# Giving every engine a written order of work in a fused graph-attention layer

## The chip, the cores and the metric

The kernel runs on one core of a Trainium2 chip. The metric is the device time of one execution in microseconds (us). The engines are TensorE (PE, with its weight loads PEld), VectorE (DVE), ScalarE (ACT), GpSimd (POOL) and SyncE (SP), which here only issues DMA transfers.

## The reference

The input x is 128 x 128 x 768, 128 graphs of 128 nodes, in float32; adj is 128 x 128 x 128. Cut to what matters:

```
h = relu(layernorm(x))                         # over the last axis, eps 1e-5
q, k, v = h @ Wq + bq, h @ Wk + bk, h @ Wv + bv  # 12 heads of 64
scores = q @ k^T / 8 + beta * adj
scores = where(adj > 0, scores, -9e15)
out = x + softmax(scores) @ v                  # heads put side by side again
```

## The kernel before

The work is cut into 32 groups of four graphs. For each group the three projections are done in three **slices**: `qk0` (q and k of the first six heads), `v`, and `qk1` (q and k of the other six). A slice is a product of 2 x 3 blocks of activations with 3 x 3 blocks of weights, each block 256 wide, and it is done with 15 block products (`PRODUCTS`) in place of 18. The inputs of these products are sums of blocks: `sum_acts` (DVE) makes the sums of activations, named S, and the sums of weights, named T, are made once.

In the qk0 and v slices each block product is itself done with 7 instead of 8 products of half blocks (`product_z`, 28 matmuls at L494). Its weights are seven 128 x 128 parts that are prepared once in group 0 (`prepare`), stored to DRAM (`kept`, L259 and L285) and loaded again for every product (`load_T`, L305), 448 KB each. A ring of five buffers (`RING`) holds them; the load for the product five places on is issued when a product has freed its buffer. The activations' inner sums, named SP, are made by POOL (`inner`, L426 to L429), four operations for each product. The results of a slice are kept in encoded form and decoded by POOL (`decode`, L537 to L540 for q and k, L548 to L553 for v) before they are used. A product's result is taken out of its PSUM bank by ACT where it is the first for an output block, and added by DVE otherwise (L519, L520); the next product of the same chain (there are four chains, each with its own banks) needs that bank free.

The qk1 slice uses plain block products (`product`, L568) with weights that stay in SBUF. Group 0 runs qk0 and v with plain weights (`plain_slice`, L768), while the weights are prepared.

Beside the slices, written into a dictionary `todo` from the number of a block product to functions, go:

- the attention of the group: `scores` (L604, L608, L611) and `attend` (L641), whose steps are put between matmuls; its end scales the result (L625), adds x on POOL (L650) and stores it (L651). The x for that is loaded by `load_xo` (L592)
- the layer norm of the next group: x is loaded in transposed blocks (`load_x`, L169), normalized by ACT (`norm`, L408) and transposed by DVE (`to_hT`, L414). From the third group on, the statistics come from x by rows (`load_halves`, `row_stats` at L383, `row_moments` at L394 and L395) and are turned to the blocks' order by 16 small transfers (`block<-row`, L399)
- the bias from adj (`load_adj` L436, `bias_1`, `bias_2`, L441 to L458).

Apart from the startup all transfers are issued by SP, in the order in which they stand in its program. The order in which the engines get these instructions is set by the framework's scheduler, by priority and its own estimate of times; `tc.issue_after` puts single instructions behind others. So products of the qk1 slice are found inside the v slice of the profile.

Of the kernel before, what the change touches and what calls it, by code (L numbers as in the profile page):

```python
# [31 lines left out]
def kernel(  # L32
# [25 lines left out]
    with tc.If(again > 0):  # L58
# [56 lines left out]
HT_AT = {"A01": 0, "A00": 1, "A11": 2, "A02": 3, "A10": 4, "A12": 9}  # L115
SUMS_AT = (5, 9, 6, 6, 7, 8, 9, 10, 11, 13, 14)
INNER_AT = ((5, (1, 11, 12)), (6, (0,)), (7, (4, 2)), (8, (5,)), (9, (6,)), (10, (8, 3, 9)), (11, (7,)), (12, (10,)),
            (14, (13, 14)))


@with_exitstack
def direct(ctx, tc, x, adj, wq, bq, wk, bk, wv, bv, beta, out, bad):
# [42 lines left out]
    def load_x(G, g, engines):  # L165
        t = home_x(G, g)
        src = x[G * GRP + g].rearrange("(b i) (a f) -> a i b f", i=SQ, a=NB)
        for a in range(NB):
            engines[a % len(engines)].dma_start(t[a * SQ:(a + 1) * SQ], src[a])  # L169
# [26 lines left out]
    def load_part(w, k, at, n, t):  # L196
        src = w.rearrange("(a c j) n -> a j c n", a=NB, j=SQ)
        for a in range(NB):
            nc.sync.dma_start(t[a * SQ:(a + 1) * SQ], src[a][:, 2 * k:2 * k + 2, at:at + n])

    def load_block(sl, k, j, t):
        if sl == "v":
            load_part(wv, k, j * 2 * P, 2 * P, t)
        else:
            for i, w in enumerate((wq, wk)):
                load_part(w, k, (j + 3 * int(sl[2])) * P, P, t[:, :, i * P:(i + 1) * P])
# [3 lines left out]
    def load_weights(sl, blocks=[f"B{k}{j}" for j in range(3) for k in range(3)]):  # L210
        for b in blocks:
            if sl == "qk1":
                t = const.tile([P, 2, H2], F32, name=f"{sl}_{HOME.get(b, b)}")
            else:
                n = nraw[0]
                nraw[0] += 1
                if n < len(PRODUCTS):
                    t = work.tile([P, GRP, P], F32, tag=f"SP{n}", name=f"{sl}_{b}", bufs=1)
                else:
                    t = work.tile([P, GRP, P], F32, tag="xo", name=f"{sl}_{b}", bufs=3)  # L220
                t = t.rearrange("p (c i) n -> p c (i n)", c=2)
            load_block(sl, int(b[1]), int(b[2]), t)
            wt[sl, b] = t
# [83 lines left out]
    load_weights("qk0", ["B00", "B10", "B20"])  # L307
    for g in range(2, GRP):
        load_x(0, g, (nc.sync,))
# [76 lines left out]
    def row_moments(G):  # L386
# [10 lines left out]
        for b in range(NB):  # L397
            for a in range(NB):
                nc.sync.dma_start(to[a * SQ:(a + 1) * SQ, b], t[b * SQ:(b + 1) * SQ])  # L399
# [39 lines left out]
    def bias_1(G, raw):  # L439
        a = work.tile([P, GRP, N], F32, tag="adjT", name=f"adjT_{G}", bufs=1)  # L440
        nc.vector.transpose(a, raw.rearrange("p g b j -> p g (b j)"))  # L441
# [3 lines left out]
        t = biasT[G] = work.tile([P, GRP, N], F32, tag="biasT", name=f"biasT_{G}", bufs=2)  # L445
        nc.gpsimd.memset(t, MASKED)
        nc.vector.copy_predicated(t, kp, a)
        if G:
            square(a)
        return a  # L450

    def square(a):
        nc.scalar.activation(a, a, AF.Square, scale=1.0005 * math.sqrt(SUM_CAP) / (BIAS_CAP * ISCALE))

    def bias_2(G, a):
# [6 lines left out]
    between = deque()  # L462
# [18 lines left out]
    def product_z(G, sl, n):  # L481
# [15 lines left out]
        load_T()  # L497
        for (r, j), sign in uses:
# [23 lines left out]
            if not left[key]:  # L522
                decode(G, sl, r, j)
        if n == mine[-1]:
            for b in banks.pop(chain):
                give(b)

# [27 lines left out]
    def product(G, sl, n, order):  # L555
# [8 lines left out]
        for i in range(2):  # L564
            for c in range(2):
# [4 lines left out]
                turn()  # L570
        for (r, j), sign in uses:
# [13 lines left out]
        if n == mine[-1]:  # L585
            give(banks.pop(chain))

# [44 lines left out]
    def attend_steps(G, oc):  # L632
# [17 lines left out]
        nc.gpsimd.tensor_add(t, t, o.rearrange("p a (b j) d -> p (a b) (j d)", j=2))  # L650
        nc.sync.dma_start(out[G * GRP:(G + 1) * GRP, :, oc * P:(oc + 1) * P].rearrange("g n d -> n g d"), t)  # L651
# [80 lines left out]
    def attention(G, u, at=AV_AT):  # L732

        todo = {}
        for i, oc in enumerate((3 * u + 2, 3 * u, 3 * u + 1)):
            todo.setdefault(at[i] - 3, []).append(lambda oc=oc: load_xo(G, oc))
            todo.setdefault(at[i], []).append(lambda oc=oc: attend(G, oc))
        return todo

    def slice_z(G, sl, todo):  # L740
        for at, n in enumerate(ZORDER):
            product_z(G, sl, n)
            for f in todo.get(at, ()):
                f()

    def slice_of(G, sl, todo, order=range(len(PRODUCTS))):
        for at, n in enumerate(order):
            product(G, sl, n, order)
            for f in todo.get(at, ()):
                f()  # L750

    def plain_slice(G, sl, todo):

        n = 0
        for r in range(2):
            for j in range(3):
# [4 lines left out]
                for at, k in [(at, k) for at in parts for k in range(3)]:  # L761
# [28 lines left out]
                    for f in todo.get(n, ()):  # L790
                        f()
                    n += 1


    adj_0 = load_adj(0)
# [96 lines left out]
    def behind_adds(f, *args):  # L892

        with tc.issue_after(added[0].ins):
            return f(*args)

    def behind_scores(f, *args):

        with tc.issue_after(taken[0].ins):
            return f(*args)  # L900

# [5 lines left out]
    early, raw = [], []  # L907
    for G in range(NG):
        todo = attention(G - 1, 1, AV_Z) if G else {}

        def then(n, f):
            todo.setdefault(n, []).append(f)

        def behind(f, *args):

            with tc.issue_after(added[G].ins):
                return f(*args)

        if G:
            for n, order in ((1, (2, 0)), (2, (1,))):  # L920
                todo.setdefault(n, []).insert(0, lambda order=order: scores(G - 1, 1, order))

        if G + 1 < NG:
            for g in range(GRP):
                then(6, lambda g=g: load_x(G + 1, g, (nc.sync,)))
                if G == 1:
                    then(11 + g, lambda g=g: behind_scores(stats, G + 1, g))
                elif G:
                    then((0, 5, 8, 11)[g], lambda g=g: load_halves(G + 1, g))
                    then((4, 7, 10, 13)[g], lambda g=g: behind(row_stats, G + 1, g))  # L930
            if G > 1:
                raw = []
                then(14, lambda: raw.append(load_adj(G + 1)))
                then(14, lambda: row_moments(G + 1))
        if not G:
            load_weights("qk1", AS_SUMMED)
            then(0, lambda: behind_rows(half, 0))
            then(3, lambda: half(1))
            then(4, lambda: half(2))
            prep = deque(prepare("qk0") + prepare("v"))  # L940

            def step(behind, count):
                for _ in range(count):
                    if prep:
                        behind(prep.popleft())

            for n in range(5, 18):
                then(n, lambda n=n: step(after, 1 + n % 2))
            plain_slice(0, "qk0", todo)
        else:  # L950
            if G == 1:
                then(4, lambda: behind_scores(bias_2, 1, early[1]))
            slice_z(G, "qk0", todo)
        todo = {1: [lambda: scores(G, 0, (2, 0))], 2: [lambda: scores(G, 0, (1,))]} if G else {}
        if G + 1 < NG:
            got = []
            at = 3 if G else 5
            for g in range(GRP):
                if not G:
                    then(g, lambda g=g: stats(G + 1, g))  # L960
                if G or g < 2:
                    then(at + 5 + g, lambda g=g: behind(norm, G + 1, g) if G > 1 else norm(G + 1, g))
            if G < 2:
                then(at, lambda: got.extend(moments_1(G + 1, 0, GRP * NB)))
                then(at + (3 if G else 2), lambda: moments_2(G + 1, 0, GRP * NB, *got[:2]))
            if G:
                then(8, lambda: got.append(behind(bias_1, G + 1, raw.pop()) if raw else bias_1(G + 1, load_adj(G + 1))))
                then(12, lambda: bias_2(G + 1, got[-1]))
            else:
                for n in range(len(SUMS_B)):  # L970
                    then(n + 3, lambda n=n: behind_adds(sum_weights, "qk1", n))
                for n in range(len(SUMS_A)):
                    then(n + 4, lambda n=n: sum_acts(0, n))
                for n in range(18):
                    then(n, lambda: step(lambda f: f(), 2))
                then(10, lambda: early.append(behind_adds(bias_1, 0, adj_0)))
        if G:
            slice_z(G, "v", todo)
        else:
            plain_slice(0, "v", todo)  # L980
        todo = attention(G, 0)
        if not G:
            todo.setdefault(SC_AT, []).insert(0, lambda: scores(0, 0))

        def transposes(n):
            with tc.issue_after(added[G].ins if G else taken[0].ins):
                to_hT(G + 1, int(n[1]), int(n[2]))

        def behind_opened(f, *args):

            with tc.issue_after(opened[0].ins):
# [175 lines left out]
```

## Time and profile before

| | |
|---|---|
| median of 2 runs (lowest, highest) | 3589.33 us (3587.52, 3591.14) |
| the profiled execution | 3600.97 us |
| its span, first to last instruction | 3599.0 us |
| granted TensorE clock, mean | 0.912 |
| PE busy | 2921.5 us, 81% |
| POOL busy | 2334.8 us, 65% |
| DVE busy | 2114.0 us, 59% |
| ACT busy | 1361.9 us, 38% |
| DMA | 660.86 MB, mean 184 GB/s, 57.6% of 16 engines |
| first matmul with prepared weights (group 1) | 206.2 us |
| first qk0 matmul of group 2 and of group 31 | 299.1 us and 3485.1 us |

Times inside the profile are microseconds from the first instruction of that execution. A line of a group reads: line of the code, engine, operation, what it writes and reads, number | busy time, mean ns of one | idle time of the engine before them and what ended it. A line of waits reads: who waits, for whom: total us, times, longest. A timeline line reads: start, duration, engine and line, what; SPq is the issue of a transfer.

### The profile page before, as it was taken

To read this page: it belongs to the slowest core of one execution; us is meant where nothing else is said; L and a number is where in the kernel's file an instruction comes from. 1 tells how busy PE (TensorE), PEld (TensorE's weight loads), DVE (VectorE), ACT (ScalarE), POOL (GpSimd) and SP (SyncE) were. 2 spreads that over 40 slices of the span, in tenths; PEclk is the share of its full clock that TensorE was granted. 3 is DMA by queue.
4 is the path that set the end of the run, shared out by engine and by line. 5 is a ranking of instruction groups with operands and counts; after the bars stand their busy time and mean duration, and the time that the engine had idled before them with its cause. 6 is when DMAs were issued, how large, how long until landed. Compare 5 with 4: busy or idle time off the path is not lost.

```text
span 3599.0 us, 114220 instructions
## 1 busy us (share of the span) xinstructions
PE 2921.5 (81%) x46385; PEld 2519.5 (70%) x46385; DVE 2114.0 (59%) x4755; ACT 1361.9 (38%) x3999; POOL 2334.8 (65%) x4146
## 2 busy tenths in 40 slices
PE   8478878778888788787787887787877878878878
PEld 7377767667677767676676777676776767776767
DVE  3556656556565566565565655565655756556655
ACT  1234343343343443334433433433344334344333
POOL 1757766568676677665686766676656867567764
PEclk9779999899999999999999999998988999999999
DMA  3485655756556656557565566565575655665644
GB/s 96 155 250 168 204 168 184 223 166 195 170 168 218 192 168 207 158 189 222 170 197 177 164 213 204 164 209 159 180 223 165 198 173 164 217 191 170 207 142 154
DMA packets 552487, 660.86 MB, mean 184 GB/s; under 512 B 126348, under 2 KB 428696, under 8 KB 551960
## 3 DMA queue, kind: packets, MB, share of 16 engines
q1 hardware_dynamic: 551632, 653.13, 57.6%
q8 instruction: 367, 6.01, 0.7%
q14 instruction: 160, 1.31, 0.1%
q10 hardware_dynamic: 328, 0.40, 0.1%
HBM read 588.78 MB, written 64.09 MB: 181 GB/s over the span
## 4 chain that ended last, share of the span: by engine, by line


## 5 line engine op out<-in xcount | busy, mean ns | idle before, releaser
L494 PE MATMUL bank<-SP,T_qk 128*64 128x128 f32 x7440 | 709.5, 288 | 46.9 <-POOL SP L428 46.9
L494 PE MATMUL bank<-T_v,SP 128*64 128x128 f32 x7440 | 679.3, 285 | 0.0
L625 ACT ACTIVATE o<-bank,sm 128x64 f32<-128x64 f32 x1524 | 348.4, 318 | 849.2 <-DVE sm L619 448.9
L494 PE MATMUL bank<-S,T_qk 128*64 128x128 f32 x4092 | 445.4, 295 | 244.3 <-DMA T_qk<-kept_qk 243.5
L494 PE MATMUL bank<-T_v,S 128*64 128x128 f32 x4092 | 432.8, 293 | 221.0 <-DMA T_v<-kept_v 219.4
L519 DVE TENSOR_TENSOR qk<-qk,bank 128x512 f32<-128x512 f32 x310 | 208.5, 672 | 559.0 <-PE bank L494 391.0
L548 POOL TENSOR_TENSOR v<-v 128x128 f32<-128x128 f32 x186 | 85.3, 459 | 681.3 <-DVE v L519 681.3
L494 PEld LDWEIGHTS bank<-SP,T_qk 128*64 128x64 f32 x7440 | 482.9, 147 | 53.0 <-POOL SP L428 53.0
L641 PEld LDWEIGHTS bank<-v,e 128*64 128x64 f32 x6048 | 407.2, 138 | 128.0 <-ACT o L625 11.6
L494 PEld LDWEIGHTS bank<-T_v,SP 128*64 128x64 f32 x7440 | 486.4, 145 | 0.0
L494 PEld LDWEIGHTS bank<-S,T_qk 128*64 128x64 f32 x4092 | 281.4, 150 | 261.5 <-issue 254.5
L494 PEld LDWEIGHTS bank<-T_v,S 128*64 128x64 f32 x4092 | 275.1, 148 | 247.0 <-DMA T_v<-kept_v 228.0
L568 PE MATMUL bank<-S,qk_T 128*64 128x256 f32 x3584 | 442.2, 380 | 2.6 <-DVE qk L583 1.7
L641 PE MATMUL bank<-v,e 128*64 128x65 f32 x6048 | 432.3, 222 | 13.2 <-ACT o L625 7.0
L537 POOL TENSOR_TENSOR qk<-qk 128x256 f32<-128x256 f32 x186 | 135.8, 730 | 325.4 <-DVE qk L519 325.2
L577 ACT ACTIVATE qk<-bank,bqk 128x256 f32<-128x256 f32 x384 | 164.2, 473 | 362.5 <-POOL v L553 158.9
L583 DVE TENSOR_TENSOR qk<-qk,bank 128x512 f32<-128x512 f32 x321 | 219.1, 683 | 137.6 <-PE bank L568 116.5
L568 PE MATMUL bank<-A,qk_T 128*64 128x256 f32 x2048 | 253.4, 384 | 48.3 <-ACT v L509 41.2
L608 DVE SCALAR_TENSOR_TENSOR e<-bank,biasT 128x512 f32<-128x512 f32 x378 | 237.9, 684 | 89.6 <-PE bank L604 88.7
L568 PE MATMUL bank<-S,qk_B 128*64 128x256 f32 x2048 | 278.8, 384 | 13.5 <-DVE qk L583 12.7
L568 PEld LDWEIGHTS bank<-S,qk_T 128*64 128x64 f32 x3584 | 231.1, 137 | 82.5 <-DVE qk L583 1.8
L408 ACT ACTIVATE x<-x,block 128x192 f32<-128x192 f32 x464 | 217.9, 536 | 138.3 <-DMA block<-row 133.2
(157 smaller groups left out, 5934.1 us busy)
## 6 DMA issues: line engine op xcount, KB each, us to landing
T_qk<-kept_qk SPq DMA_DIRECT2D x465, 448.0 KB, 5.0
T_v<-kept_v SPq DMA_DIRECT2D x465, 448.0 KB, 4.7
x<-in_x_dram SPq DMA_DIRECT2D x504, 96.0 KB, 2.8
xo<-in_x_dram SPq DMA_DIRECT2D x189, 256.0 KB, 5.3
out_dram<-xo SPq DMA_DIRECT2D x189, 256.0 KB, 2.6
half<-in_x_dram SPq DMA_DIRECT2D x232, 192.0 KB, 4.7
adj<-in_adj_dram SPq DMA_DIRECT2D x128, 64.0 KB, 3.1
block<-row SPq DMA_DIRECT2D x464, 1.0 KB, 1.7
```

Source lines behind the costliest of these rows:

```text
L408: nc.scalar.activation(t, t, AF.Relu, bias=shift[G, n], scale=rstd[G, n])
L494: nc.tensor.matmul(p[z // 4][q:q + HD, z % 4, :], lhs[:, q:q + HD], rhs, start=(first and z % 4 == 0), stop=True, skip_group_check=True)
L519: nc.vector.tensor_tensor(t[:, 0:4], t[:, 0:4], p[0], op)
L537: e.tensor_tensor(t[:, 1:4:2], t[:, 1:4:2], twice(0), ALU.add)
L548: e.tensor_tensor(v[:, 0:2, 0:HD], heads(0), heads(3), ALU.add)
L568: nc.tensor.matmul(p[q:q + HD, i, :], lhs[:, q:q + HD], rhs, start=(first and i == 0 and c == 0), stop=(c == 1), skip_group_check=True)
L577: opened[0] = nc.scalar.activation(t[:, i, :], p[:, i, :], AF.Identity, bias=bqk[:, i, oc:oc + 1], scale=float(sign))
L583: added[G] = nc.vector.tensor_tensor(t[:, :, cols], t[:, :, cols], p[:, :, cols], ALU.add if sign > 0 else ALU.subtract)
L608: taken[0] = nc.vector.scalar_tensor_tensor(e, ps[oc, i].rearrange("p (g n) -> p g n", g=GRP), SCORE_CAP * ISCALE, biasT[G], op0=ALU.min, ...
L625: nc.scalar.activation(o[:, b], pa[:, b, 0:HD], AF.Copy, scale=t[:, 1, b:b + 1])
L641: nc.tensor.matmul(pa[q:q + HD, 2 * g + i, :], es[G, oc, i][:, 2 * r + g, q:q + HD], vt[G, "v", r, h // 4][:, 4 * g + h % 4, :], start=Tru ...
```

## The change

The framework's scheduler keeps only the first slice of group 0 and the last slice of the last group. Between them, under `tc.manual_schedule()`, every engine runs its instructions in the order in which the program states them. A slice is run by slots, one for each block product: first the product's matmuls and (in qk0 and v) the issue of the next T load, then the slot's `todo`, then what earlier slots put off, then the taking out of the product's result, then what is marked "post":

```
+    def later(f, slots=1):
+        while len(deferred) < slots:
+            deferred.append([])
+        deferred[slots - 1].append(f)
+
+    def overdue():
+        if deferred:
+            for f in deferred.popleft():
+                f()
...
+    def run(products, todo):
+        for at, steps in enumerate(products):
+            next(steps)
             for f in todo.get(at, ()):
                 f()
+            overdue()
+            next(steps)
+            for f in todo.get((at, "post"), ()):
+                f()
```

The decoding of an output block, the addition of x and the store are put off by one, one and two slots:

```
             if not left[key]:
-                decode(G, sl, r, j)
+                later(lambda r=r, j=j: decode(G, sl, r, j))
...
-        nc.gpsimd.tensor_add(t, t, o.rearrange("p a (b j) d -> p (a b) (j d)", j=2))
-        nc.sync.dma_start(out[G * GRP:(G + 1) * GRP, :, oc * P:(oc + 1) * P].rearrange("g n d -> n g d"), t)
+
+        def add():
+            nc.gpsimd.tensor_add(t, t, o.rearrange("p a (b j) d -> p (a b) (j d)", j=2))
+
+        def send():
+            nc.sync.dma_start(out[G * GRP:(G + 1) * GRP, :, oc * P:(oc + 1) * P].rearrange("g n d -> n g d"), t)
+
+        later(add)
+        later(send, 2)
```

x is loaded for two graphs by one set of four transfers, a weight block by two transfers of 128 partitions instead of four of 32 (the first three blocks on the queues of SP and ACT), and the row statistics are turned by way of DRAM:

```
-    def load_x(G, g, engines):
-        t = home_x(G, g)
-        src = x[G * GRP + g].rearrange("(b i) (a f) -> a i b f", i=SQ, a=NB)
+    def load_x(G, r):
+        for g in range(2):
+            home_x(G, 2 * r + g)
+        src = x[G * GRP + 2 * r:G * GRP + 2 * r + 2].rearrange("g (b i) (a f) -> a i (g b) f", i=SQ, a=NB)
         for a in range(NB):
-            engines[a % len(engines)].dma_start(t[a * SQ:(a + 1) * SQ], src[a])
+            nc.sync.dma_start(xp[G, r][a * SQ:(a + 1) * SQ], src[a])
...
-        src = w.rearrange("(a c j) n -> a j c n", a=NB, j=SQ)
-        for a in range(NB):
-            nc.sync.dma_start(t[a * SQ:(a + 1) * SQ], src[a][:, 2 * k:2 * k + 2, at:at + n])
+        src = w.rearrange("(a c j) n -> c a j n", a=NB, j=SQ)
+        for c in range(2):
+            engine.dma_start(t[:, c], src[2 * k + c][:, :, at:at + n])
...
-        for b in range(NB):
-            for a in range(NB):
-                nc.sync.dma_start(to[a * SQ:(a + 1) * SQ, b], t[b * SQ:(b + 1) * SQ])
+        turned = dram.tile([SQ, NB, 2 * GRP], F32, name=f"turned_{G}")
+        nc.sync.dma_start(turned.rearrange("i b s -> b i s"), t.rearrange("p s g -> p (s g)"))
+        nc.sync.dma_start(to.rearrange("p b s g -> p (b s g)"),
+                          turned.rearrange("i b s -> i (b s)")[None].to_broadcast([NB, SQ, NB * 2 * GRP]))
```

The bias is cut into four steps (`bias_steps`). The slots of the regular groups, from the third on (`then(slot, function, ...)`, `activations` and `attention` fill the same dictionary):

```
+    def activations(G, first):
+        for name, at in (("A01", 3), ("A00", 5), ("A02", 6), ("A11", 9), ("A10", 17), ("A12", 24)):
+            if at >= 15:
+                then(at - 15, to_hT, G, int(name[1]), int(name[2]))
...
+        for n, at in enumerate((2, 10, 3, 5, 6, 7, 11, 12, 13, 14)):
+            then(at, sum_acts, G, n)
+        for n, at in ((0, 3), (1, 3), (2, 4), (11, 4), (12, 5), (4, 6), (5, 7), (6, 8), (8, 10), (3, 11), (7, 12), (9, 13),
+                      (10, 14), (13, 14)):
+            then(at, inner, G, n)
...
# qk0 of group G (more: a further group follows)
+        then(0, sum_acts, G, 10)
+        then(1, inner, G, 14)
+        for n, order in ((1, (2, 0)), (2, (1,))):
+            then((n, "post"), scores, G - 1, 1, order)
+        attention(G - 1, 1, AV_Z)
...
+        elif more:
+            then(0, row_moments, G + 1)
+            then(0, add_raw, G + 1)
+            bias(G + 1, 3, 5, 6, 12)
# v of group G
+        for n, order in ((1, (2, 0)), (2, (1,))):
+            then((n, "post"), scores, G, 0, order)
+        if more:
+            for g in range(GRP):
+                then((0, 2, 4, 6)[g], norm, G + 1, g)
+            for name, at in (("A01", 4), ("A00", 5), ("A02", 6), ("A11", 9)):
+                then(at, to_hT, G + 1, int(name[1]), int(name[2]))
...
+                then(13, load_halves, G + 2, 0)
# qk1 of group G
+        attention(G, 0, AV_AT)
+        activations(G + 1, False)
+        if G + 2 < NG:
+            for g, at in enumerate((1, 4, 8, 12)):
+                then(at, row_stats, G + 2, g)
+                if g < 3:
+                    then(at, load_halves, G + 2, g + 1)
+            for r, at in enumerate((6, 11)):
+                then(at, load_x, G + 2, r)
```

`add_raw` issues the four loads of adj; `attention(G, u, at)` puts the load of x for the sum three slots ahead of each of its three `attend`, at slots 7, 9, 12 (`AV_Z`) and 5, 8, 11 (`AV_AT`). Before, x of the next group was loaded at slot 6 of qk0, the row halves at slots 0, 5, 8 and 11 and `row_moments` and the adjacency at slot 14 of qk0, the normalizations stood at slots 8 to 11 and the bias at 8 and 12 of v.

## The prediction

> **What bounds the kernel now.** I read the page's table of engines first. TensorE (PE) is busy 81% of the span, so some 680 us of idle time are to be found. The page's list of groups says what ends them: the first matmuls of a block product wait for the load of a prepared weight T, 244 us in the qk0 slices and 219 us in the v slices.
>
> ```profile
> PE 2921.5 (81%) x46385; PEld 2519.5 (70%) x46385; DVE 2114.0 (59%) x4755; ACT 1361.9 (38%) x3999; POOL 2334.8 (65%) x4146
> ...
> L494 PE MATMUL bank<-S,T_qk 128*64 128x128 f32 x4092 | 445.4, 295 | 244.3 <-DMA T_qk<-kept_qk 243.5
> L494 PE MATMUL bank<-T_v,S 128*64 128x128 f32 x4092 | 432.8, 293 | 221.0 <-DMA T_v<-kept_v 219.4
> ```
>
> Then the busy times by stretch for one middle group, from its first qk0 matmul to the next group's, cut where PE stops and starts (columns: stretch, length, busy us of PE, PEld, DVE, ACT, POOL, granted clock, DMA share, GB/s):
>
> ```profile
> 1835.90:1848.90 13.00, 11.35 (x240) 10.14 (x235) 6.75 (x13) 9.49 (x30) 12.61 (x26) 1.00 0.34 95
> 1848.90:1856.60 7.70, 0.03 (x2) 0.06 (x2) 2.00 (x5) 0.20 (x1) 5.28 (x11) 0.68 0.76 223
> 1856.60:1877.40 20.80, 20.80 (x376) 20.63 (x378) 13.35 (x37) 7.39 (x28) 11.79 (x16) 0.87 0.94 314
> 1877.40:1889.90 12.50, 11.21 (x242) 10.28 (x240) 9.04 (x27) 7.17 (x17) 8.68 (x13) 1.00 0.67 191
> 1889.90:1903.40 13.50, 3.80 (x36) 2.02 (x31) 0.83 (x2) 7.71 (x17) 0.00 (x0) 0.85 0.25 68
> 1903.40:1920.50 17.10, 16.97 (x278) 16.58 (x280) 12.26 (x24) 3.62 (x9) 10.12 (x21) 0.92 0.89 301
> 1920.50:1945.90 25.40, 25.40 (x312) 17.88 (x310) 21.21 (x46) 7.07 (x24) 24.46 (x45) 1.00 0.34 104
> 1835.90:1945.90 110.00, 89.55 (x1470) 77.59 (x1467) 65.43 (x149) 42.65 (x125) 72.94 (x130) 0.92 0.60 187
> 243.50:270.40 26.90, 26.63 (x514) 25.66 (x511) 20.67 (x48) 16.10 (x35) 17.69 (x28) 1.00 0.90 283
> 270.40:299.10 28.70, 28.70 (x342) 20.02 (x339) 22.21 (x48) 8.74 (x28) 27.60 (x54) 1.00 0.35 106
> ```
>
> A group takes 110 us and has two holes of 7.7 us, in the second and fifth rows. In neither is the DMA system full (223 and 68 GB/s, where 314 is reached right after), so the loads come late because they are issued late. The last two rows are the first regular group's v and qk1 slices, which have no hole: 26.9 and 28.7 us. The issues on SyncE's queue (SP) tell why:
>
> ```profile
> 1839.12 0.41 SPq L651 DMA_DIRECT2D out_dram<-xo  x1
> ...
> 1846.95 0.40 SPq L651 DMA_DIRECT2D out_dram<-xo  x1
> ...
> 1852.13 0.40 SPq L651 DMA_DIRECT2D out_dram<-xo  x1
> 1852.63 0.94 SPq L305 DMA_DIRECT2D T_qk<-kept_qk  x2
> ...
> 1887.81 11.29 SPq L399 DMA_DIRECT2D block<-row  x16
> 1899.19 1.95 SPq L305 DMA_DIRECT2D T_v<-kept_v  x4
> ```
>
> SP issues in order. In qk0 three stores of results wait, one after the other, for GpSimd's (POOL's) addition, and the T loads stand behind them until 16.7 us into the slice. In v the sixteen transfers of the row statistics take 11.3 us of issue. SP's waits carry the first cause over the whole run:
>
> ```profile
> SPq L651 <- POOL SP L426: 614.7, 59, 28.2
> ```
>
> POOL is the source: its timeline runs without a gap from 1799.95 to 1853.81, 53.9 us: the decoding of v (L548 to L553), the inner sums (L426 to L429) and three additions (L650).
>
> **Without any hole** a group costs PE: 15 z products of 28 matmuls, 1.53 us each by the timeline, are 22.9 us for qk0 and the same for v; scores 2 x 3.1; 15 qk1 products of 1.73 are 25.9; attention 2 x 2.7. That is 28.7 + 26.0 + 28.7 = 83.4 us, so 26.6 of the 110 are lost.
>
> **The row statistics: 16 transfers become 2.** v and qk1 together took 1945.9 - 1877.4 = 68.5 us, of which 54.7 are work and 13.8 are lost: 1.3 us for a decode, 2.0 and 7.7 us of idle time, the rest at half clock after the hole. The 11.3 us of issue go. New are two issues, and a wait between them, since the second reads from DRAM what the first wrote. No row shows such a pair; the 1 KB pieces land 1.7 us after their issue, a 256 KB store after 2.6. I take 1.7, the size nearest. The Trainium skill ("DMA: Bandwidth & Descriptors", section "Two DMAs through the same engine are not ordered") says that the issuing engine must wait for the first one's semaphore, which speaks against the change. No run here shows it yet; by it SP stands still for a landing in each group, and with no such wait the sum below would be 29 x 1.7 = 49 us less.
>
> **Where the pair now stands** matters more. It moves from the end of qk0 to the start of qk0, behind POOL's power (1.01 us) and product (0.20), and these stand behind POOL's whole stream. So I lay the stream into the new order. The decoding of v starts after the eviction of v's eighth product; PE then has some 11.3 us of v and 28.9 of qk1 left, 40.2 us. The stream is 19.6 (v) + 14 inner sums of 2.09 = 29.3 + 3 x 1.27 + 1.2 = 53.9 us. It runs over by 13.7 us: SP can issue the first of the pair 13.7 us into qk0, the second 1.7 later, then four adjacency loads (0.5 each), and only then, at about 17.9, the T load of the seventh product; PE starts 3.9 us after the issue (1852.63 to 1856.57), at 21.8. The sixth product's load stands behind the third store, whose addition comes two inner sums, the power and the product earlier (5.4 us): issue at 8.7, start at 12.6. PE has work until 10.7 (five products and the scores). So there are two holes again, 1.9 and 7.7 us, and **qk0 takes** 21.8 + 9 x 1.53 + 2.7 + 2.6 for half clock (5.3 us at half speed in the old slice) + 0.5, since DVE's adjacency transpose waits in order for those loads ahead of an eviction = 41.4 us, against 41.5 now. The hole stays, its cause now the statistics instead of the stores. Bounds: 28.7 (nothing held) to 45 (pair landing like a store, T load 5 us).
>
> **v in the new order.** The T loads come in time (26.9 us without a hole). But ACT takes four normalizations of 4 x 0.536 = 2.1 us, at slots 0, 2, 4 and 6, ahead of the evictions of the same slots. ACT's work to slot 6 is 8.6 + 6 x 0.87 (first evictions) + 6 x 0.635 (exponentials) = 17.6 us, and PE's there is 6 slots and the scores, 12.3. Followed product by product, PE waits about 0.5 and 0.5 at the scores for the decode, 1.4 at slot 6 and 1.8 at slot 8: **30.2 us**. Bounds: 26.9, and 34 if all of ACT's surplus is paid. qk1: DVE has 6.8 (evictions) + 8.2 (sums) + 5.2 (row statistics, moved here) + 4.0 (maxima and reciprocals of the softmax sums) + 1.4 (transposes) = 25.6 us in 28.7; the halves of x that it reads are issued ahead of the stores that wait. I take 28.9, with 31 as the end.
>
> **A middle group** is then 41.4 + 30.2 + 28.9 = 100.5 us against 110.0, 9.5 less. From the first qk0 of 299.1 us to that of 3485.1 there are 29 groups: 275 us.
>
> **x**: 16 issues of 96 KB a group, half of them in qk0, become 8 of 192 KB in qk1. The DMA system is used 0.34 in qk1, and in qk0 SP waits anyway: nothing gained or lost; without that wait, the 8 issues of 0.47 taken out of qk0 would be worth 3.8 us a group. The bias work goes to qk0, 4.4 us of DVE under a hole that stays: nothing. The addition and the store, put off by one and two slots, only move SP's wait, which is in the sum above.
>
> **The start.** 180 weight transfers become 90. SP issues one each 0.47 us (10 in 4.66 at 60.00), and the first store of a prepared weight goes out at 100.59, behind all of them; POOL, out of ring buffers until then, is idle from 52.9 to 103.5 but for one operation, then busy to 206, when the first qk0 with prepared weights begins. With 90 fewer issues the stores start some 42 us earlier, and POOL's work follows; 12 fewer for x of groups 0 and 1 make 48. I take 50 with the scheduler's gaps (10 to 12 us waits of PE near 180 and 200) partly gone. Bounds: 0, if the fixed order holds the preparation elsewhere, and 75, where PE's own work ends (87.8 + 28.7 + scores and attention gives 130). **The last group** has no statistics to hold SP: its qk0 falls from 41.2 to about 35, 6 us.
>
> **The sum**: 3601.0 of the profiled execution - 275 - 50 - 6 = 3270; the shown runs' median is 11.7 below that execution, which makes **3258**.
>
> **Rivals.** (1) SP is not held in qk0: POOL's overrun is small since PE no longer outruns it, or the pair is issued early. Then 28.7 + 27.5 + 28.8 = 85 us a group: 3601 - 29 x 25 - 50 - 6 - 12 = 2808; with one hole of half the length about 2970. For it: POOL's busy time is 73 us a group and fits into 85. Against it: the 53.9 us stream is in one piece, and it has 40 us. (2) The change does not do what it says: the order only moves the holes, v included, and the group stays at 109: 3510 to 3590. Against it: 11.3 us of issue leave SP. (3) **Slower: POOL's stream grows.** Beside DVE's sums with two inputs from SBUF, POOL's 0.46 us operations take 0.90 (1817.85 to 1821.30, DVE at 0.94). The new order spreads eleven such sums over the whole qk1 slice, where the inner sums run. Each us more on the stream moves the seventh product's T load by one; from 9.5 us more (60 inner operations at 0.68 instead of 0.52) the gain of a group is gone. Were all at 0.90, it is 22.8 us: 123 us a group, 3601 + 29 x 13 - 68 = 3910. Against it: in the trace only some ten in sixty take 0.9. The Trainium skill ("GPSIMD Engine Reference", section "1. Specifications") says that POOL shares its SBUF interfaces with VectorE and contends with instructions of two SBUF inputs; the trace agrees, with 0.90 beside 0.46.
>
> **How the numbers follow.** Forecast 0.56 (own range 3130 to 3420, from the bounds of qk0, v and the start); rival 1 0.22 (2800 to 3050); rival 2 0.08; rival 3 0.14. The range 2900 to 3590 leaves out about 0.06 below and 0.14 above. Two per cent (72 us), about what a measurement can tell here, puts faster at 0.78, same at 0.08, slower at 0.14.
>
> **What would show it.** Right: no run of sixteen L399 issues, v without a wait for T; in qk0 SP's first wait of length is the statistics' store behind POOL, with a hole of 7 to 9 us before the seventh product; short waits of PE for ACT in the middle of v; prepared weights stored from about 58 us. Wrong: qk0 near 30 us (rival 1), POOL's inner operations above 0.6 us on average (rival 3), or PE waiting in qk1 for DVE, which I cost at 0.2 us and which would come from the halves of x landing late.

## The result and the profile after

The changed kernel takes **3209.19 us** (median of 2 runs, 3206.68 to 3211.70) against 3589.33: a ratio of 0.894, 95% interval 0.890 to 0.898. The forecast was 3258, with 3130 to 3420 as its own range and 2900 to 3590 as the range with the rivals. The profiled execution took 3211.70 us with a span of 3209.8; the mean granted clock rose from 0.912 to 0.946.

The span cut at the same points as before, so that the sum of the prediction can be checked term by term:

| stretch | before, us | after, us | difference | predicted |
|---|---|---|---|---|
| to the first qk0 of group 2 (start and group 1) | 299.1 | 308.0 | +8.9 | -50 |
| from there to the first qk0 of group 31, 29 groups | 3186.0 | 2798.3 | -387.7 | -275 |
| the rest, the last group | 113.9 | 103.5 | -10.4 | -6 |
| span | 3599.0 | 3209.8 | -389.2 | -331 |

The total came within 1.5% of the forecast in part by luck, because two terms were missed in opposite directions. A group fell from 109.9 to 96.5 us, not to 100.5, and the start became longer, not shorter.

The page's table of engines and its groups of the first matmuls of a block product (busy, mean ns, then the idle time ahead and what ended it), kernel after:

```profile
PE 2830.4 (88%) x46385; PEld 2462.4 (77%) x46385; DVE 2155.4 (67%) x4755; ACT 1338.4 (42%) x3999; POOL 2331.3 (73%) x4146
...
L499 PE MATMUL bank<-S,T_qk 128*64 128x128 f32 x4092 | 453.5, 295 | 255.2 <-DMA T_qk<-kept_qk 159.5
L499 PE MATMUL bank<-T_v,S 128*64 128x128 f32 x4092 | 405.7, 274 | 18.8 <-ACT v L513 14.8
```

The 221.0 us of idle time ahead of the v products are 18.8 now. The 244.3 us of qk0 are still 255.2. So one hole went and the other stayed, as forecast. In the stretches of a middle group, cut at the same kind of places as before (columns: stretch, length, busy us of PE, PEld, DVE, ACT, POOL, granted clock, DMA share, GB/s):

```profile
1755.57:1768.50 12.93, 11.76 (x248) 10.86 (x246) 9.24 (x16) 8.94 (x26) 12.49 (x23) 1.00 0.31 86
1768.50:1777.00 8.50, 1.20 (x22) 0.95 (x18) 1.91 (x4) 1.30 (x4) 2.35 (x6) 0.79 0.49 121
1777.00:1795.30 18.30, 18.16 (x350) 18.19 (x352) 13.58 (x37) 6.62 (x25) 12.23 (x18) 0.91 0.98 329
1795.30:1822.50 27.20, 26.58 (x521) 25.41 (x518) 20.98 (x44) 15.45 (x38) 17.58 (x32) 1.00 0.82 265
1822.50:1851.30 28.80, 28.80 (x343) 20.12 (x341) 20.70 (x51) 9.43 (x33) 25.39 (x50) 1.00 0.62 165
```

The first three rows are qk0, 39.7 us with a hole in its second row; the last two are v and qk1, in which PE hardly stops. SP's queue in the same qk0 slice (start, duration, engine and line, what; a duration over several issues takes in the waits between them):

```profile
1756.26 8.09 SPq L664 DMA_DIRECT2D out_dram<-xo  x2
1764.44 0.46 SPq L301 DMA_DIRECT2D T_qk<-kept_qk  x1
1768.76 0.57 SPq L393 DMA_DIRECT2D turned<-row  x1
1770.72 0.52 SPq L394 DMA_DIRECT2D block<-turned  x1
1771.33 2.02 SPq L432 DMA_DIRECT2D adj<-in_adj_dram  x4
1773.45 1.85 SPq L301 DMA_DIRECT2D T_qk<-kept_qk  x4
```

This is the order that the prediction laid out: the third store (the second of the first line), one T load, the pair, the adjacency, then the T load of the seventh product, on which PE starts at 1777.14. SP's waits over the whole run (total us, times, longest) say for whom it stood:

```profile
SPq L664 <- POOL xo L661: 430.1, 143, 20.6
SPq L664 <- POOL SP L422: 272.2, 40, 8.0
...
SPq L393 <- POOL SP L422: 117.2, 29, 4.2
SPq L394 <- DMA turned<-row: 38.1, 29, 1.3
```

### The profile page after: what moved, and what is told of

The parts are those of the page before. It is cut to its first block, busy times and chain, and to the rows that moved or that the text cites. A ratio compares the mean times of both kernels' runs of the same rounds, so it can differ in the third digit from the quotient of the medians.

```text
span 3209.8 us, 113028 instructions
## 1 busy us (share of the span) xinstructions
PE 2830.4 (88%) x46385; PEld 2462.4 (77%) x46385; DVE 2155.4 (67%) x4755; ACT 1338.4 (42%) x3999; POOL 2331.3 (73%) x4146
## 4 chain that ended last, share of the span: by engine, by line
## 5 line engine op out<-in xcount | busy, mean ns | idle before, releaser
L499 PE MATMUL bank<-S,T_qk 128*64 128x128 f32 x4092 | 453.5, 295 | 255.2 <-DMA T_qk<-kept_qk 159.5
L499 PE MATMUL bank<-T_v,SP 128*64 128x128 f32 x7440 | 647.7, 273 | 0.0
L650 PEld LDWEIGHTS bank<-v,e 128*64 128x64 f32 x6048 | 427.2, 137 | 108.4 <-issue 1.0
L499 PEld LDWEIGHTS bank<-SP,T_qk 128*64 128x64 f32 x7440 | 496.5, 147 | 0.5 <-issue 0.5
L499 PEld LDWEIGHTS bank<-T_v,SP 128*64 128x64 f32 x7440 | 460.0, 137 | 0.0
L650 PE MATMUL bank<-v,e 128*64 128x65 f32 x6048 | 446.1, 221 | 0.9 <-issue 0.9
L499 PE MATMUL bank<-T_v,S 128*64 128x128 f32 x4092 | 405.7, 274 | 18.8 <-ACT v L513 14.8
L525 DVE TENSOR_TENSOR v<-v,bank 128x512 f32<-128x512 f32 x310 | 212.0, 684 | 156.9 <-PE bank L499 94.5
L499 PEld LDWEIGHTS bank<-T_v,S 128*64 128x64 f32 x4092 | 260.1, 137 | 33.5 <-ACT v L513 23.9
L525 DVE TENSOR_TENSOR qk<-qk,bank 128x512 f32<-128x512 f32 x310 | 209.3, 675 | 98.7 <-PE bank L499 97.4
L661 POOL TENSOR_TENSOR xo<-xo,o 128x512 f32<-128x512 f32 x189 | 254.6, 1347 | 11.7 <-ACT o L634 11.7
```

What stands on the lines that cost most here:

```text
L499: nc.tensor.matmul(p[z // 4][q:q + HD, z % 4, :], lhs[:, q:q + HD], rhs, start=(first and z % 4 == 0), stop=True, skip_group_check=True)
L525: nc.vector.tensor_tensor(t[:, 0:4], t[:, 0:4], p[0], op)
L650: nc.tensor.matmul(pa[q:q + HD, 2 * g + i, :], es[G, oc, i][:, 2 * r + g, q:q + HD], vt[G, "v", r, h // 4][:, 4 * g + h % 4, :], start=Tru ...
```

## The experiments

Eleven kernels, each timed beside the kernel before, whose median was 3588 to 3595 us in these runs; the ratio is to that. `group` is the mean of the 29 middle groups, the slices are medians of middle groups, all in us. The last column is the start of the first qk0 of group 2.

| kernel | time | ratio, interval | group | qk0 | v | qk1 | group 2 at |
|---|---|---|---|---|---|---|---|
| before | 3589 | 1 | 109.9 | 41.7 | 67.9 with qk1 | | 299.1 |
| after | 3209 | 0.894 (0.890-0.898) | 96.5 | 40.0 | 27.3 | 28.7 | 308.0 |
| b_pair | 3280 | 0.915 (0.912-0.917) | 99.1 | 38.0 | 32.1 | 28.7 | 299.1 |
| a_16 | 3430 | 0.957 (0.954-0.959) | 104.0 | 48.1 | 27.3 | 28.7 | 304.3 |
| a_sched | 3505 | 0.977 (0.974-0.980) | 106.5 | 41.2 | 37.2 | 28.7 | 308.0 |
| a_pair | 3059 | 0.853 (0.851-0.855) | 91.5 | 35.1 | 27.6 | 28.7 | 304.4 |
| a_both | 3006 | 0.836 (0.832-0.839) | 89.4 | 33.3 | 27.4 | 28.7 | 306.7 |
| a_all | 2980 | 0.829 (0.825-0.832) | 88.8 | 33.1 | 27.4 | 28.7 | 302.2 |
| a_bias | 2915 | 0.811 (0.808-0.815) | 86.4 | 30.4 | 27.0 | 28.7 | 301.2 |
| a_start | 3217 | 0.895 (0.891-0.898) | 96.5 | 40.0 | 27.3 | 28.7 | 310.5 |
| a_four | 3211 | 0.893 (0.890-0.896) | 96.7 | 40.2 | 27.3 | 28.7 | 297.0 |
| a_start2 | 3179 | 0.885 (0.882-0.888) | 96.3 | 39.8 | 27.3 | 28.7 | 285.1 |
| a_top | 2895 | 0.805 (0.803-0.808) | 86.5 | 30.5 | 27.2 | 28.7 | 281.3 |

### Which part of the change makes the gain

**b_pair**: the kernel before with the row statistics turned by two transfers through DRAM, nothing else, in the scheduler's order.

```diff
-        for b in range(NB):
-            for a in range(NB):
-                nc.sync.dma_start(to[a * SQ:(a + 1) * SQ, b], t[b * SQ:(b + 1) * SQ])
+        turned = dram.tile([SQ, NB, 2 * GRP], F32, name=f"turned_{G}")
+        nc.sync.dma_start(turned.rearrange("i b s -> b i s"), t.rearrange("p s g -> p (s g)"))
+        nc.sync.dma_start(to.rearrange("p b s g -> p (b s g)"),
+                          turned.rearrange("i b s -> i (b s)")[None].to_broadcast([NB, SQ, NB * 2 * GRP]))
```

> The kernel before with one thing changed: the row statistics go by the two transfers through DRAM in place of the sixteen; order and slots stay the scheduler's. Theory (SP's issue time is what made the hole in v): the pair takes some 2.6 us of SP in place of 11.3, so the T loads of v go out 8.7 us earlier and the hole of 7.7 us and its half clock go: 9 to 10 us a group, about 3320 us. Rival (the written order makes the gain, the transfers little): 3520 or more.

**a_16**: the opposite edit, in the kernel after: the sixteen small transfers again, in the place where the pair stands.

> The changed kernel with the sixteen transfers of the row statistics in place of the two, at the same place. Theory: in qk0 the T loads stand 8.7 us longer behind them on SP, so the hole in qk0 grows by 8 to 9 us: 29 x 8.5 = 247 us more, about 3455. Rival (the hole in qk0 is set by POOL's sums or by DVE's wait for the adjacency, not by SP's T loads): under 3300.

**a_sched**: the kernel after, its text and its slots unchanged, with the scheduler setting the order of the engines.

```diff
-    ordered.enter_context(tc.manual_schedule())
```

> The changed kernel without the fixed order: the same program text with the framework's scheduler ordering all engines. Theory (what stands ahead of the T loads on SP counts, and the scheduler also sends stores and statistics ahead of them): v without a hole, qk0 with one of 7 to 10 us, 3250 to 3400. Rival (the fixed order is what cures v): 3500 or more.

The pair alone gives 308 us of the 380 (3588 to 3280), and without the pair the rest gives 158. The two overlap: both shorten the v slice, the pair by freeing SP, the order by moving the statistics out of v's way (v takes 27.3 us in a_16 as well). In b_pair, PE still waits 80.1 us over the run for the weights of v, and v takes 32.1 us; qk0 fell from 41.7 to 38.0, which its theory did not have and which was not followed further. In the stated order the sixteen transfers sit in qk0, where SP is already late. In one middle group they take 10.0 us to issue (1774.68 to 1784.70), where the pair takes 2.5 with its wait (1768.76 to 1771.24), and the group takes 7.5 us more (104.0 against 96.5). That is 221 us over the run. VectorE's wait for the adjacency, which stands behind the same transfers, grows with it, from 314.6 to 533.7 us, so a_16 does not tell its share from that of the T loads.

a_sched missed the theory (3250 to 3400) and came out where its rival had it (3500 or more): without the stated order v is not cured. It takes 37.2 us with 7.5 of idle time, and PE waits there for VectorE's evictions, where the kernel after has 18.8 us of idle time ahead of the v products for all causes:

```profile
PE bank L499 <- DVE v L525: 161.2, 54, 5.5
```

So the new places of the work, with the new loads of x and of the weights, are no better than the old ones if the scheduler still orders each engine: the kernel is 225 us slower than b_pair. The slots and the stated order belong together. What in the scheduler's order makes VectorE late was not followed further.

### Where the rest of qk0 goes

**a_pair**: in the kernel after, the pair is issued at slot 7 of qk0; its sums stay at slot 0. So the T loads of the sixth and seventh product are ahead of it on SP's queue.

```diff
-        turned = dram.tile(...)
-        nc.sync.dma_start(turned..., t...)
-        nc.sync.dma_start(to..., turned...)
+        def turn_rows():
+            ...
+        rows[G, "turn"] = turn_rows
...
             then(0, row_moments, G + 1)
+            then(7, lambda G=G: rows[G + 1, "turn"]())
```

> The changed kernel with the two transfers of the row statistics issued at slot 7 of qk0 in place of slot 0; the sums on DVE and POOL stay at slot 0, the adjacency's loads too. Theory: the seventh product's T load goes out right behind the third store and the adjacency's loads, 11.4 us into the slice in place of 17.9, and DVE's wait for the adjacency ends near 14.7: qk0 32 to 34 us in place of 39.9, so 29 x 6 to 7.5: 2990 to 3035. Rival (POOL is the bound once SP is free): the wait comes back as PE waiting for POOL's sums or decodes, above 3130.

**a_both**: a_pair with the adjacency loads in qk1, one group earlier.

```diff
-            then(0, add_raw, G + 1)
...
+            then(13, add_raw, G + 2)
```

> The kernel after with the pair at slot 7 of qk0 and, besides, the four adjacency loads moved to slot 13 of qk1, one group earlier. With the pair moved alone, 3059 us, qk0 took 35.1 us with 4.1 idle, and VectorE still waited 179 us in all for the adjacency, whose loads stand on SyncE's queue behind the second store's wait. Theory (what holds qk0 is whatever stands on SyncE's queue behind a wait for GpSimd): the T loads of the sixth and seventh product no longer pass four issues, about 2 us, and VectorE's transposes do not wait: qk0 31 to 32.5, 2.6 to 4 us less in each of 29 groups, 2940 to 2985 us. Rival (GpSimd's stream itself is what is late, the stores still wait for it, and the place of the adjacency is nothing): 3040 to 3065.

**a_all**: a_both with the store put off.

```diff
-        later(send, 2)
+        later(send, 6)
```

> As the kernel with the pair at slot 7 and the adjacency in qk1, with the store of the result put off by six slots in place of two, so that no store on SyncE's queue waits for GpSimd while T loads stand behind it. Theory: no hole in qk0 is left, 28.7 to 29.5 us; with v 27.3 and qk1 28.7 a group is 85 us: 3209 - 29 x 11.2 = 2870 to 2920 us, which is rival 1 of the prediction, 85 us a group, made true. Rival (GpSimd, busy 70 us a group with a stream of 54 that overruns the end of qk1 by 13 us, or VectorE, becomes the bound): qk0 stays at 31 or more, 2950 or more.

a_pair takes 5.0 us from a group where 6 to 7.5 were expected, a_both 2.1 more where 2.6 to 4 were expected. In both, the stores still wait for POOL (333 and 244 us over the run in a_both), so T loads behind them still come late.

a_all removes that wait (60 and 45 us are left), yet gains only 0.7 us a group. The sizes are the rival's. Its mechanism was close but not the same, and the trace names the actual one. PE's longest wait in qk0 is now for ScalarE. Waits of PE between 600 and 2900 us of a_all:

```profile
PE bank L503 <- ACT qk L523: 57.3, 25, 2.5
```

The timelines of POOL, VectorE and ScalarE at that place, in the qk0 slice that begins at 1279.97, one fence for each engine:

```profile
1295.40 0.53 POOL L447 MEMSET biasT<- 128x512 f32 x1
```

```profile
1295.96 0.73 DVE L452 COPY_PREDICATED biasT<-kp,adjT 128x512 f32<-128x512 uint8 x1 [2.59 <-POOL biasT L447]
```

```profile
1296.73 0.63 ACT L453 ACTIVATE adjT<-adjT 128x512 f32<-128x512 f32 x1 [3.46 <-DVE biasT L452]
1297.26 0.35 ACT L522 ACTIVATE qk<-bank,bqk 128x128 f32<-128x128 f32 x1
1297.51 0.48 ACT L523 ACTIVATE qk<-bank 128x384 f32<-128x384 f32 x1
```

The memset of the bias tile stands in POOL's stated order behind the same overrunning stream. VectorE's masked copy waits for it, ScalarE's square of the adjacency waits for the copy, and ScalarE's eviction of a product stands behind the square, though PE's matmuls had all ended at 1295.64. PE waits 2.41 us for that bank. The end of POOL's stream reaches PE by way of two engines that stand idle for it.

**a_bias**: a_all with the copy and the square four slots later.

```diff
-            bias(G + 1, 3, 5, 6, 12)
+            bias(G + 1, 3, 5, 10, 12)
```

> The kernel with the pair at slot 7, the adjacency in qk1 and the store put off by six slots took 2980 us, with a wait of 2.4 us left in qk0: TensorE waits for an eviction by ScalarE, which stands behind ScalarE's square of the adjacency (slot 6), which waits for VectorE's copy under a mask, which waits for GpSimd's memset of the bias tile at the end of GpSimd's stream, at 15.4 us of qk0. This kernel is the same with the copy and the square at slot 10 in place of 6. Theory (the order now stated lets GpSimd's overrun reach TensorE through ScalarE's place in order, and nothing else does): the wait goes, qk0 32.6 to 29.5 us, 29 x 2.4 to 3.1: 2890 to 2915 us. Rival (GpSimd, busy 73 us of 88, is so late that the next thing behind it holds TensorE as long: the decoding of q and k for the scores): 2950 to 2985.

One number changed, and the kernel is 65 us faster: qk0 falls to 30.4 us, and the time is at the upper end of what the theory gave (2915.47 against 2890 to 2915). Of the 2.4 us a group, 1.3 are idle time of PE in qk0 (2.4 in the mean in a_all, 1.1 in a_bias). Most of the rest is clock: in 16 of the 29 qk0 slices of a_all the mean granted clock is 0.95, with a stretch of 3.41 us at 0.5 that begins near the end of the wait, and in a_bias in none. POOL has the same work in all these kernels (2340 us busy in a_both, 2338 in a_top). So POOL was not the bound. What cost the time was what stood in order behind its late end.

### The start

Three timeline lines of SP, kernel after: the loads of the v weights, the first store of a prepared weight, the x of group 1.

```profile
42.25 24.09 SPq L195 DMA_DIRECT2D v_B<-in_L_gnn_Wv_dram  x18
...
97.95 0.61 SPq L255 DMA_DIRECT2D kept_qk<-prep_qk  x1
98.61 5.39 SPq L165 DMA_DIRECT2D x<-in_x_dram  x8
```

Eighteen issues of 128 KB take 24.09 us, 1.34 each. Before, thirty-six of 64 KB took 18.11, 0.50 each. The waits of the kernel after between 40 and 200 us show who stood meanwhile:

```profile
DVE st L325 <- DMA x<-in_x_dram: 55.3, 1, 55.3
```

```profile
PE bank L336 <- DVE st L325: 51.3, 1, 51.3
```

```profile
POOL prep_qk L276 <- DMA kept_qk<-prep_qk: 54.7, 2, 48.7
```

**a_start**: the loads of the qk1 weights behind the x of group 1. **a_four**: four transfers of 32 partitions for each weight block again, so 180 in place of 90.

```diff
# a_start
-    load_weights("qk1", AS_SUMMED)
...
     for r in range(2):
         then(6, load_x, 1, r)
+    then(6, load_weights, "qk1", AS_SUMMED)
# a_four
-        src = w.rearrange("(a c j) n -> c a j n", a=NB, j=SQ)
-        for c in range(2):
-            engine.dma_start(t[:, c], src[2 * k + c][:, :, at:at + n])
+        src = w.rearrange("(a c j) n -> a j c n", a=NB, j=SQ)
+        for a in range(NB):
+            engine.dma_start(t[a * SQ:(a + 1) * SQ], src[a][:, 2 * k:2 * k + 2, at:at + n])
```

> The kernel after with the loads of the qk1 weights moved behind the first loads of x for group 1 (slot 6 of the first slice). In the kernel after, the x of group 1 is issued at 98.6 to 103.7 us, behind those weights; VectorE waits for it from 52.4 to 107.7 and TensorE for VectorE from 79.0 to 130.3. Theory (the start was missed because the order now stated puts VectorE's layer norm of group 1 ahead of the sums of the plain v slice, and its x is on SyncE's queue behind the weights): the 51 us wait of TensorE shrinks to under 15, the first qk0 of group 2 comes 20 to 45 us earlier (308 before), 3165 to 3190 us. Rival (GpSimd's preparation and its stores, not x, set the first product with prepared weights, at 203 us): it stays at 200 to 205, group 2 at 300 to 308, 3200 to 3210.

> The kernel after with each weight block loaded by four transfers of 32 partitions again, in place of two of 128: 180 issues in place of 90 at the start, all else as it is. The prediction put 42 us on these 90 issues at 0.47 each. Theory (an issue of the larger kind costs as much as two of the small ones, so the count said nothing): the weights are issued in about the same time, the first store of a prepared weight at 95 to 105 us, group 2 at 300 to 315, 3200 to 3220 us. Rival (each issue costs 0.47 as predicted, and the gain was eaten by the wait for x alone): 90 more issues put everything at the start back by about 40 us: 3240 to 3255.

a_four settles the count: with 90 more issues the first store goes out earlier, at 92.82 us, group 2 begins at 297.0, both a little ahead of what the theory gave, and the time is the same. Most of the 11 us won at the start are lost again in the groups, of 96.7 us against 96.5, and in the last one. In it the v weights are issued like this:

```profile
40.55 18.34 SPq L195 DMA_DIRECT2D v_B<-in_L_gnn_Wv_dram  x36
```

a_start's theory fell, and its rival held: the x of group 1 was issued 30 us earlier, but the first product with prepared weights came at 207.3 us, and nothing was gained. SP's lines show why:

```profile
66.70 1.26 SPq L255 DMA_DIRECT2D kept_qk<-prep_qk  x1
68.01 10.04 SPq L165 DMA_DIRECT2D x<-in_x_dram  x8
...
110.77 1.80 SPq L255 DMA_DIRECT2D kept_qk<-prep_qk  x3
```

The first store left at 66.7, but the second still stood behind the qk1 weights until 110.8. The preparation needs those stores to get its buffers back, so POOL and VectorE stood until then (36.4 us in the longest wait of each), and with them the plain v slice: PE's wait for VectorE is still 53.1 us.

**a_start2**: the qk1 weights one block at a time at slots 0 to 8 of the plain v slice, behind these stores.

```diff
-    load_weights("qk1", AS_SUMMED)
...
     todo.clear()
+    for n, b in enumerate(AS_SUMMED):
+        then(n, load_weights, "qk1", [b])
     for g in range(GRP):
         then(g, stats, 1, g)
```

> The kernel after with the nine blocks of the qk1 weights loaded at slots 0 to 8 of the plain v slice, behind x of group 1 and behind the first stores of prepared weights. With them behind x alone the first store went out at 66.7 us in place of 98.0, but the second still stood behind these weights, at 110.8, and nothing was gained. Theory (GpSimd's preparation is about 95 us of work in a row and sets the first product with prepared weights; it starts when its first stores have left SyncE's queue): stores from 67 to 80 us on, the first product with prepared weights at 165 to 180 us in place of 203, 3170 to 3190 us. Rival (VectorE, which sums the qk1 weights in its stated order, now waits for these loads, or TensorE's plain products for VectorE): 195 or later, 3200 to 3215.

```profile
78.41 2.11 SPq L255 DMA_DIRECT2D kept_qk<-prep_qk  x3
```

The second to fourth stores now go out from 78.4 us, the first product with prepared weights comes at 182.8 us instead of 202.7 (165 to 180 were expected), and the whole is 30 us faster.

**a_top**: a_bias and a_start2 together.

> All moves together: the pair at slot 7, the adjacency in qk1, the store put off by six slots, the bias's copy and square at slot 10, and the qk1 weights behind the first stores. Theory: a group of 85.5 to 86.5 us and a start shorter by 20 to 35 us, 2860 to 2900 us. Rival (what is gained at the start or in qk0 is waited for elsewhere): above 2930.

**2894.75 us** (2887.97 to 2899.48), a ratio of 0.805 (0.803 to 0.808) to the kernel before and some 314 us under the kernel after. Its page and one stretch of the length of a group:

```profile
PE 2758.5 (95%) x46385; PEld 2400.7 (83%) x46385; DVE 2166.4 (75%) x4755; ACT 1338.4 (46%) x3999; POOL 2337.8 (81%) x4146
```

```profile
1000.00:1086.50 86.50, 83.76 (x1451) 73.02 (x1449) 66.56 (x148) 41.79 (x125) 72.98 (x130) 1.00 0.78 234
```

PE is busy 83.76 of 86.50 us. The working of the prediction gave 83.4 us for a group without any hole.

## Why the prediction was right, and where its terms were wrong

**SP in qk0: right, to within 0.7 us at each step.** Against the start of the slice (1755.57), predicted and measured: issue of the third store 8.7 and 8.4; first of the pair 13.7 and 13.2; second 1.7 and 1.96 later; T load of the seventh product 17.9 and 17.9; PE again 21.8 and 21.6; holes 1.9 and 7.7, and 1.2 and 7.4. qk0 came to 39.7 us here and 40.0 in the median, against 41.4. What was too high is the part after the hole: 19.1 us with its half clock, and 0.5 for VectorE, measured as 18.2. The granted clock of that row is 0.91, so the half clock costs about 1.6 us, not 2.6.

The hole has a second cause that was priced at 0.5 us: VectorE stands in order for the adjacency (314.6 us in 30 waits), so in some groups the eviction and not the T load ends last (PE behind L526: 83.8 us). The holes have the forecast length all the same: the adjacency and the T load leave the same place of SP's queue, 2 us apart.

**The wait inside the pair: right, and a little shorter.** SP waited 38.1 us in 29 groups, 1.3 us each, where the prediction had 29 x 1.7. The Trainium skill ("DMA: Bandwidth & Descriptors", section "Two DMAs through the same engine are not ordered") says that the issuing engine must wait for the first one's semaphore; the trace agrees, with that wait.

**"v in the new order": the direction right, the size wrong.** The term of 30.2 us was mis-sized; it is 27.3. It had 4.2 us of waits of PE, 3.2 of them for ScalarE; those for ScalarE are 14.8 us over the whole run, 0.5 in a group. ScalarE's work to slot 6 ends 16.0 us into the slice, not 17.6, since its operations overlap (four normalizations in 1.85 us, not 2.1). That leaves ScalarE still 3.7 us behind PE's 12.3, and PE does not wait for it: the surplus of one engine over another in a stretch is not yet a wait. The likely reason, argued and not tried, is that a late eviction holds a bank that PE takes up again only some products later. This term is 2.9 of the 4.0 us by which the group was missed, 84 us of the run; qk0 is most of the rest.

**"The start": wrong in its mechanism.** The step read "With 90 fewer issues the stores start some 42 us earlier". It took the price of an issue, 0.47 us, from transfers of 32 partitions and gave it to those of 128 partitions, which move twice as much. These are issued 0.6 to 0.8 us apart with 64 KB and 1.34 apart with 128 KB, and the first store moved from 100.59 to 97.95, not to about 58. The bound given for this case, "0, if the fixed order holds the preparation elsewhere", has the right size, but its mechanism is at most a part. The stated order does have the layer norm of group 1 (VectorE's L325, PE's L336), whose x comes behind the qk1 weights, ahead of the end of the plain v slice, yet an earlier x alone gained nothing (a_start). What the first product with prepared weights follows is the second store, which stands behind the weights too, as it did before the change: it comes 96.2 us after that store before, 98.0 in the kernel after, 97.2 in a_four, 96.5 in a_start and 104.4 in a_start2, while the store itself moves from 110.77 (a_start) to 78.41 us (a_start2). Of the 59 us by which the start was missed, 46.5 are this: -3.5 us to the first product with prepared weights, not -50. The other 12.4 are group 1, which had no term of its own: it takes 105.3 us against 92.9 (qk0 44.7 against 37.3, v 31.9 against 26.9); why was not followed.

**x and the bias "nothing": right in this kernel, for the reason given.** The bias work was priced at nothing "under a hole that stays". When a_all took the hole away, its place cost 2.4 us a group, as a_bias shows. x was not tried by itself.

**The rivals.** Rival 1 (SP not held, 85 us a group) did not come about, but its price was nearly right: a_top, which frees SP in qk0, has 86.5 us a group. Rival 2, only moved holes, 3510 to 3590, is nearly the time that a_sched gave, where PE waits for VectorE's evictions in v. Rival 3 did not appear: POOL's inner operations take 472 to 582 ns in the mean in the kernel after (L422 to L425 on S), 460 to 562 before.

## What to carry to other kernels

In an in-order queue, price a step by everything that stands behind it. Here 308 of the 380 us could be had by taking sixteen issues out of the way of the T loads. Most of the 314 us that were still to be had came from transfers, an eviction and a copy that stood behind something that waited for POOL, while POOL itself was not the bound. An edit that costs nothing under a hole has to be priced again once the hole is gone. Where the program states the order, look at the first wait of each engine in each slice, and move what waits behind what others need.

## What the runs showed of the hardware beyond the expected

- **The cost of issuing a transfer depends on its shape and on what stands before it.** The weight loads of 32 partitions, of 32 and 64 KB, are issued 0.47 to 0.51 us apart. Those of 128 partitions, whose source is four runs of rows, are issued 0.6 apart with 64 KB where few stand together (a_start2 at 96.4 to 99 us), 0.8 apart with 64 KB in a row of 32 (kernel after, 72 to 98 us) and 1.34 apart with 128 KB in a row of eighteen. In these two rows 83 and 97 GB/s move (72 to 98 and 42 to 66 us), and 64 KB in 0.8 us and 128 KB in 1.34 us are some 80 and 98 GB/s: the issue keeps step with the data, so it seems to wait for them, which was not tried. Between 50 and 60 us 89 GB/s move, against 128 (before) and 138 (a_four) with the small ones. The four x transfers issued behind the first of them take 7.07 us (kernel after) instead of 1.95 (a_four). A rule that fits is in the Trainium skill ("DMA: Bandwidth & Descriptors", section "Why a DMA increments its semaphore by 16 and not by 1"): the number of DMA engines of a transfer is the largest one, up to 16, that divides the slowest dimension of both sides. That dimension is 4 in the source of the new form and 32 on both sides of the old, so 4 engines in place of 16. The traces agree: they hold four packets of 4 bytes for each load of the new form (129 for 31 loads between 72.1 and 97.9 us, kernel after) and sixteen for each of the old (1136 for 70 between 64.8 and 100 us, before).
- **The same pair waits 1.3 us or 4.7 us.** Issued into a queue that had stood still, the second waits 38.1 us in 29 groups for the first; behind T loads in flight 135.2 us (a_pair). SP is held 3.4 us longer in each group. That this is why a_pair came out above its range was not tried.
- **A hole is paid for again in the clock.** With a hole of 7.4 us the granted clock is 0.79 in its row and 0.91 over the 18.3 us after it. Shorter ones can cost clock too: in a_all 15 waits of 2.2 to 2.5 us in qk0 go with a stretch of 3.41 us at half clock, and others of the same length do not. In a_bias and a_top, where no single wait of PE between 300 and 2800 us is longer than 1.9 us, there is no such stretch in that time, and the mean of the run is 0.984 and 0.987.
